# Sparse graph attention on one core: part one as a software pipeline, biases filled into PSUM by ScalarE, and a small tile of 12 slots first

## The chip, the cores and the metric

The kernel runs on one core of one Trainium2 chip. The metric is the device time of one execution in microseconds; of the kernel before it is the median of three runs. The engines are called PE (TensorE, matrix products), DVE (VectorE), ACT (ScalarE), POOL (GpSimd, which also issues the indirect DMAs) and SP (SyncE, which issues DMAs). PE reads its stationary operand by weight loads, which the profile lists as PEld.

## The reference

A layer norm with relu, then graph attention over the neighbours that an adjacency matrix lists, then a residual.

```python
# x: 3327 x 1024, adj: 3327 x 3327 int32 (symmetric, with the diagonal, about 0.5% ones), weights 1024 x 1024
h = jnp.maximum(_layernorm(x, axis=-1), 0.0)
f = h @ Wf + bf
g = h @ Wg + bg
e = relu(f @ g.T)
scores = jnp.where(adj > 0, e, -9e15)
attention = softmax(scores, axis=1)
out = x + attention @ (h @ W + bW)
```

## The kernel before

The kernel uses that a row has few neighbours (37 at most, 17 in the mean). It never forms f, g or the full score matrix. With A = Wf Wg^T the score of nodes i and j is a dot of q_i = h_i A + ... with h_j, and since attention weights sum to 1, attention @ (h W + bW) is (attention @ h) W + bW.

Part one runs over 26 tiles of 128 rows. It loads adj and x, makes h and stores it in DRAM (`hd`), turns each adjacency row into a list of neighbour numbers (`pay`, stored as `pd`), and makes A meanwhile. The list comes from the eight greatest of each of 16 segments of (adj times column number), from which five rounds take the 40 greatest.

```python
def degrees(t):                                   # per tile; ACT, then POOL
    ...
        nc.scalar.activation(r[:n, b:e], a[:n, b:e], AF.Relu, accum_out=to)
        nc.gpsimd.tensor_mul(r[:n, b:e], r[:n, b:e], iotaj[:n, b:e])
def edges(t, r):                                  # DVE
    for s in range(SEG):                          # SEG = 16
        nc.vector.max(cand[:n, s * 8 : s * 8 + 8], r[:n, s * SW : min(N, (s + 1) * SW)])
    ...
    for i in range(0, KM, 8):                     # KM = 40
        nc.vector.max(lst[:n, i : i + 8], cand[:n])
        if i + 8 < KM:
            nc.vector.match_replace(cand[:n], lst[:n, i : i + 8], cand[:n], 0.0)
    ...
for t in range(NT):                               # NT = 26
    r = degrees(t)
    normed(t)                                     # load x, mean, variance, h, store hd
    edges(t, r)
    if t >= LAG: counted(t - LAG)
    ...
    if t < KD: load_Wg(t)
    elif t < 2 * KD: make_A(t - KD)
```

Then the nodes are sorted by degree on DVE and PE (`counted`, ranks, one-hot products), which gives `perm`: slot s holds the 128 nodes of rank 128 s and up. CAPS[s] is the greatest number of neighbours in slot s:

```python
CAPS = [37, 25, 23, 22, 21, 21, 20, 20, 19, 19, 18, 18, 17, 17, 17, 16, 16, 15, 15, 15, 14, 14, 13, 13, 12, 11]
```

Part two runs over the slots, two tiles prepared ahead. For each slot POOL gathers the lists and the h rows of its nodes, PE makes q, and for each neighbour k POOL gathers a row of h for every node, DVE takes the dot, a softmax follows (in two halves where CAPS is over 16), and the rows are summed by their weights, on DVE or on ACT and PE. PE multiplies the sum by W; x is gathered onto the result by an accumulating DMA; the result is scattered to `out`.

```python
def prepare(s):
    gather(pi, pd[:, :], perm[:, s : s + 1])      # lists;  psp has 3 buffers
    gather(hp, hd[:, :], perm[:, s : s + 1])      # own rows; 2 buffers of their own
    transposed2(hT, hp)
    for o in range(0, QW, QB):                    # three q blocks of 342
        for k in range(KD):
            nc.tensor.matmul(ps[:, :QB], hT[:, k, :], A_sb[:, k, o : o + QB], start=(k == 0), stop=False)
        nc.tensor.matmul(ps[:, :QB], ones3, v3[:, o : o + QB], start=False, stop=True)   # bias of q, bf16 in 3 terms
        nc.scalar.copy(q[:, o : o + QB], ps[:, :QB])
    nc.vector.tensor_copy(df, pi[:, KM : KM + 1])
    nc.vector.tensor_scalar(bads[...], df[...], float(CAPS[s]), None, op0=ALU.is_gt)
    ...
def dot(s, k):                                    # G has 25 buffers
    gather(g, hd[:, :], e["pi"][:, k : k + 1])
    nc.vector.tensor_tensor_reduce(junk, g, e["q"][:, :D], 1.0, e["q"][:, D : D + 1], ...)
def on_tensor(s, k0, k1):                         # which rows are summed by ACT and PE
    m = min(max(0, CAPS[s] - 13), k1 - k0 - 2)
    ...
def project(s):
    ...
        for k in range(KD):
            nc.tensor.matmul(ps, yT[:, k, :], W_sb[:, k, o * CB : (o + 1) * CB], start=(k == 0), stop=False)
        nc.tensor.matmul(ps, ones3, bW3[:, o * CB : (o + 1) * CB], start=False, stop=True)   # bias bW
        nc.scalar.copy(r[:, o * CB : (o + 1) * CB], ps)
    gather(r, x[:, :], perm[:, s : s + 1], compute_op=ALU.add)
```

A dense path, taken only if some row doesn't fit CAPS or a segment has over eight neighbours, stands behind a branch and isn't run on these data.

Of the kernel before, what the change touches and what calls it, by code (L numbers as in the profile page):

```python
# [18 lines left out]
EPS = 1e-5  # L19
# [3 lines left out]
NBIN = 64  # L23

CAPS = [37, 25, 23, 22, 21, 21, 20, 20, 19, 19, 18, 18, 17, 17, 17, 16, 16, 15, 15, 15, 14, 14, 13, 13, 12, 11]
ONE_CHUNK = 16
# [263 lines left out]
def edge_path(ctx: ExitStack, tc: tile.TileContext, x, adj, Wf, bf, Wg, bg, W, bW, out, flag):  # L290
# [9 lines left out]

    nc = tc.nc
# [10 lines left out]
    PW = KM + 1  # L312
# [14 lines left out]
    pd = dram.tile([N, PW], I32, name="pd")  # L327

    ident = const.tile([P, P], FP, name="ident")
    make_identity(nc, ident)  # L330
    eps = const.tile([P, 1], FP, name="eps")
    nc.gpsimd.memset(eps, EPS)
    iotak = const.tile([P, KM], FP, name="iotak")
    nc.gpsimd.iota(iotak, pattern=[[1, KM]], base=0, channel_multiplier=0, allow_small_or_imprecise_dtypes=True)
    ones3 = const.tile([3, P], BF, name="ones3")
    nc.gpsimd.memset(ones3, 1.0)
    bads = const.tile([P, NT + 2], FP, name="bads")
# [7 lines left out]
    v3 = wts.tile([3, QW], BF, name="v3")  # L345
    nc.gpsimd.memset(A_sb[:, :, D:], 0.0)
    nc.gpsimd.memset(v3[:, D:], 0.0)
    bW3 = wts.tile([3, O], BF, name="bW3")


    with ExitStack() as part1:
        pool1 = lambda name, bufs, **kw: part1.enter_context(tc.tile_pool(name=name, bufs=bufs, **kw))
        c1 = pool1("c1", 1)
        wrow = pool1("wrow", 3)
        wT = pool1("wT", 2)
        ln = pool1("ln", 5)
        lnj = pool1("lnj", 1)
        kpool = pool1("key", 4)
        cpool = pool1("cand", 2)
        p_tr = pool1("p_tr", 2, space=PSUM)  # L360
        p_mm = pool1("p_mm", 2, space=PSUM)
        p_u = pool1("p_u", 1, space=PSUM)
        p_c = pool1("p_c", 1, space=PSUM)
        p_v = pool1("p_v", 1, space=PSUM)

        iotaj = c1.tile([P, N], FP, name="iotaj")
        nc.gpsimd.iota(iotaj, pattern=[[1, N]], base=1, channel_multiplier=0, allow_small_or_imprecise_dtypes=True)
        iotap = c1.tile([P, P], FP, name="iotap")
        nc.gpsimd.iota(iotap, pattern=[[1, P]], base=0, channel_multiplier=0, allow_small_or_imprecise_dtypes=True)

        held = p_c.tile([P, NBIN + KM], FP, name="held")
        iotad, lst = held[:, :NBIN], held[:, NBIN:]
# [10 lines left out]
        deg = c1.tile([P, NT], FP, name="deg")  # L383
# [4 lines left out]
        nc.gpsimd.memset(deg, 1.0)  # L388
        nc.gpsimd.memset(cnt, 1.0)
# [5 lines left out]
        def normed(t):  # L395

            n = rows(t)
            xt = ln.tile([P, D], FP, name="xt")
            for a, m in pieces(t):
                nc.sync.dma_start(xt[a : a + m], x[t * P + a : t * P + a + m, :])  # L400
            rstd = ln.tile([P, 1], FP, name="rstd")
            nmr = ln.tile([P, 1], FP, name="nmr")
            if t % 2:
                st = ln.tile([P, D // CB, 6], FP, name="st")
                for c in range(D // CB):
                    nc.vector.bn_stats(st[:n, c, :], xt[:n, c * CB : (c + 1) * CB])
                mv = ln.tile([P, 2], FP, name="mv")
                nc.vector.bn_aggr(mv[:n], st[:n])
                nc.scalar.activation(nmr[:n], mv[:n, 0:1], AF.Copy, scale=-1.0)
                nc.scalar.activation(rstd[:n], mv[:n, 1:2], AF.Sqrt, bias=eps[:n])  # L410
            else:
                sums = ln.tile([P, 2], FP, name="sums")
# [6 lines left out]
            nc.vector.reciprocal(rstd[:n], rstd[:n])  # L419
            nc.scalar.activation(nmr[:n], nmr[:n], AF.Copy, scale=rstd[:n])  # L420
            nc.scalar.activation(xt[:n], xt[:n], AF.Relu, bias=nmr[:n], scale=rstd[:n])
            for a, m in pieces(t):
                nc.scalar.dma_start(hd[t * P + a : t * P + a + m, :], xt[a : a + m])

        def degrees(t):
            n = rows(t)
            r = kpool.tile([P, N], FP, name="r")
            a = r.bitcast(I32)
            for b, m in pieces(t):
                nc.sync.dma_start(a[b : b + m], adj[t * P + b : t * P + b + m, :])  # L430

            cuts = [0, SEG // 2 * SW, N] if t >= NT - 2 else [0, N]
            for i, (b, e) in enumerate(zip(cuts, cuts[1:])):
                to = deg[:n, t : t + 1] if not i else half[:n]
                nc.scalar.activation(r[:n, b:e], a[:n, b:e], AF.Relu, accum_out=to)  # L435
                nc.gpsimd.tensor_mul(r[:n, b:e], r[:n, b:e], iotaj[:n, b:e])  # L436
                if i:
                    nc.scalar.activation(deg[:n, t : t + 1], deg[:n, t : t + 1], AF.Identity, bias=half[:n])
            return r

        def edges(t, r):

            n = rows(t)
            cand = cpool.tile([P, SEG * 8], FP, name="cand")
            for s in range(SEG):
                nc.vector.max(cand[:n, s * 8 : s * 8 + 8], r[:n, s * SW : min(N, (s + 1) * SW)])  # L446
            pos = cpool.tile([P, SEG * 8], BF, name="pos")
            nc.vector.tensor_scalar(
                pos[:n], cand[:n], 0.0, None, op0=ALU.is_gt, op1=ALU.add, accum_out=cnt[:n, t : t + 1]
            )  # L450
            for i in range(0, KM, 8):
                nc.vector.max(lst[:n, i : i + 8], cand[:n])
                if i + 8 < KM:
                    nc.vector.match_replace(cand[:n], lst[:n, i : i + 8], cand[:n], 0.0)
            nc.vector.tensor_scalar(lst[:n], lst[:n], float(N), 1.0, op0=ALU.min, op1=ALU.max)
            nc.vector.tensor_scalar(pay[:n, t, :KM], lst[:n], -1.0, None, op0=ALU.add)
            dg = cpool.tile([P, 1], FP, name="dg")
            nc.vector.tensor_scalar(dg[:n], deg[:n, t : t + 1], float(NBIN - 1), None, op0=ALU.min)
            nc.vector.tensor_copy(pay[:n, t, KM : KM + 1], dg[:n])
            nc.vector.tensor_scalar(oh[:n, t, :], iotad[:n], dg[:n], None, op0=ALU.is_equal)  # L460
# [23 lines left out]
        def transposed(to, of):  # L484

            for g in range(0, KD, 4):
                ps = p_tr.tile([P, 4, P], FP, name="ps_tr")
                for k in range(4):
                    nc.tensor.transpose(ps[:, k, :], of[:, (g + k) * P : (g + k + 1) * P], ident)
                nc.scalar.copy(to[:, g : g + 4, :], ps)  # L490

        WgT = c1.tile([P, KD, D], FP, name="WgT")
        bfT = c1.tile([P, KD], FP, name="bfT")
        bgT = c1.tile([P, KD], FP, name="bgT")
        v_ps = p_v.tile([P, KD], FP, name="v_ps")
        cols = c1.tile([P, 2 * KD + 1], FP, name="cols")
        terms = c1.tile([P, 3, 2 * KD + 1], BF, name="terms")
        identb = c1.tile([P, P], BF, name="identb")
        nc.vector.tensor_copy(identb, ident)
        nc.gpsimd.memset(cols, 0.0)  # L500
        nc.gpsimd.dma_start(bfT, bf.rearrange("(k p) -> p k", p=P))
        nc.gpsimd.dma_start(bgT, bg.rearrange("(k p) -> p k", p=P))
        nc.gpsimd.dma_start(cols[:, KD : 2 * KD], bW.rearrange("(k p) -> p k", p=P))

        def load_Wg(c):
            wr = wrow.tile([P, D], FP, name="wr")
            nc.sync.dma_start(wr, Wg[c * P : (c + 1) * P, :])
            transposed(WgT[:, :, c * P : (c + 1) * P], wr)

        def make_A(c):  # L510

            wr = wrow.tile([P, D], FP, name="wr")
            nc.sync.dma_start(wr, Wf[c * P : (c + 1) * P, :])
            WfT = wT.tile([P, KD, P], FP, name="WfT")
            transposed(WfT, wr)
            for o in range(OH):
                ps = p_mm.tile([P, CB], FP, name="ps_A")
                for k in range(KD):
                    nc.tensor.matmul(  # L519
                        ps, WfT[:, k, :], WgT[:, k, o * CB : (o + 1) * CB], start=(k == 0), stop=(k == KD - 1)  # L520
# [34 lines left out]
        for t in range(NT):  # L555
# [3 lines left out]
            if t >= LAG:  # L559
                counted(t - LAG)  # L560
# [300 lines left out]
```

## Time and profile before

| | |
|---|---|
| Time, median of 3 (lowest, highest) | 1366.73 us (1366.68, 1373.93) |
| Span of the profiled execution | 1370.1 us |
| Mean granted PE clock | 0.939 of full |
| DVE, PE busy | 1218.5 us, 1154.2 us |
| POOL, ACT busy | 875.0 us, 489.2 us |
| Moved by DMA | 372.52 MB, mean 272 GB/s |
| Ranking chain on DVE | 272.3 to 284.7 us |
| First dot of part two | 314.4 us |
| Last sum on DVE | ends 1329.4 us |

In the profile a group is read as line, engine, operation, output<-input, shapes, count, then the busy time and the mean of one in ns, then the idle time of its engine just before it and what ended that idle time. "issue" is idle time for which the profile shows no releaser. PE runs an fp32 product of 128 rows in two passes, so its counts are twice those of the code. Busy shares are means over the span; the two parts have different limits, so the tables by stretches of time say more than the totals.

### The profile page before, as it was taken

The page shows a single profiled execution, that of the slowest core. Times are in us where ns is not written, and L with a number is a line of the kernel's source. Part 1 is how long each engine was busy: PE and PEld are TensorE (multiplying, and loading weights), DVE is VectorE, ACT ScalarE, POOL GpSimd, SP SyncE. Part 2 cuts the span into 40 slices and gives each one's busy share as a digit, 9 for nine tenths or more (in the row PEclk, how much of TensorE's full clock was granted, in tenths as well). Part 3 has the DMA queues.
Part 4 walks back from the last instruction along what each step waited for, and adds up shares of the span by engine and source line. Part 5 has one row for each costly group of instructions (what it writes and reads, how often), then busy time and mean ns, then how long its engine had stood idle before and what let it go on. Part 6 is the DMA issues. An engine that isn't in the chain of part 4 may idle for free.

```text
span 1370.1 us, 14184 instructions
## 1 busy us (share of the span) xinstructions
PE 1154.2 (84%) x4355; PEld 676.0 (49%) x4355; DVE 1218.5 (89%) x2595; ACT 489.2 (36%) x774; POOL 875.0 (64%) x628
## 2 busy tenths in 40 slices
PE   4669899246467998999999999999979999999784
PEld 3545454124244564656555555555545555555331
DVE  4888888928869999999999899999999999999970
ACT  6677676501042542344433233333322222221110
POOL 7787778435456766677667767776656667666411
PEclk9999999568689999999999999999999999999897
DMA  9887898268558989898989988988877889888612
GB/s 367 356 336 281 320 351 276 68 257 327 172 166 302 348 294 320 299 334 292 309 290 311 303 269 312 302 294 296 272 240 250 255 281 306 272 271 285 198 32 63
DMA packets 97711, 372.52 MB, mean 272 GB/s; under 512 B 14269, under 2 KB 14685, under 8 KB 94298
## 3 DMA queue, kind: packets, MB, share of 16 engines
q0 software_dynamic: 79552, 286.85, 62.4%
q1 hardware_dynamic: 10860, 70.49, 13.6%
q10 hardware_dynamic: 7212, 14.18, 2.9%
q8 instruction: 36, 0.59, 0.2%
q14 instruction: 51, 0.41, 0.1%
HBM read 343.67 MB, written 27.80 MB: 271 GB/s over the span
## 4 chain that ended last, share of the span: by engine, by line
PE 43%; issue 14%; DVE 9%; DMA 4%; POOL 4%; ACT 2%; POOLq 0%; ACTq 0%; DVEq 0%
PE ps_q L666 18%; PE ps_o L758 17%; PE yT_ps L724 6%; DVE G L746 5%; DMA G<-hd,pi 4%; POOL G L637 3%; DVE junk L683 3%; PE ps_q L667 1%; PE ps_o L759 1%; ACT hT L650 1%; DMA pi<-pd,perm 1%; PE ps_t L649 1%; DVE sc L683 1%; POOL res L637 0%; ACT q L668 0%
## 5 line engine op out<-in xcount | busy, mean ns | idle before, releaser
L637 POOL DMA_INDIRECT G<-hd,pi x468 | 541.2, 1156 | 220.2 <-issue 93.5
L683 DVE CUSTOM_DVE_ANT_0 junk<-G,q 128x1024 bf16<-128x1024 f32 x468 | 599.4, 1281 | 35.3 <-ACT q L668 18.1
L666 PE MATMUL ps_q<-A_sb,hT 128*128 128x342 f32 x1248 | 399.2, 467 | 59.4 <-ACT q L668 41.8
L746 DVE SCALAR_TENSOR_TENSOR G<-G,sc 128x1024 f32<-128x1024 f32 x320 | 410.8, 1284 | 4.6 <-ACT G L744 4.1
L758 PE MATMUL ps_o<-W_sb,yT 128*128 128x512 f32 x832 | 374.8, 604 | 4.4 <-ACT yT L753 4.4
L666 PEld LDWEIGHTS ps_q<-A_sb,hT 128*128 128x128 f32 x1248 | 231.8, 194 | 177.6 <-ACT q L668 43.7
L758 PEld LDWEIGHTS ps_o<-W_sb,yT 128*128 128x128 f32 x832 | 156.5, 192 | 195.4 <-issue 182.3
L436 POOL TENSOR_TENSOR r<-r,iotaj 128x3327 f32<-128x3327 f32 (+4 forms) x28 | 188.6, 6743 | 66.6 <-ACT r L435 51.7
L724 PE MATMUL yT_ps<-ident,G 128*128 128x128 f32 x1184 | 146.2, 279 | 24.7 <-DVE sc L708 8.2
L446 DVE MAX8 cand<-r 128x8 f32<-128x208 f32 (+2 forms) x416 | 134.4, 361 | 35.2 <-POOL r L436 35.2
L724 PEld LDWEIGHTS yT_ps<-ident,G 128*128 128x128 f32 x1184 | 133.8, 143 | 41.8 <-issue 15.7
L760 ACT COPY res<-ps_o 128x512 f32<-128x512 f32 x52 | 30.4, 585 | 298.9 <-PE ps_o L759 298.9
L740 ACT ACTIVATE G<-G,sc 128x1024 f32<-128x1024 f32 x122 | 129.2, 1135 | 0.0
L668 ACT COPY q<-ps_q 128x342 f32<-128x342 f32 x78 | 33.5, 447 | 244.8 <-DVE sc L683 135.9
L519 PE MATMUL ps_A<-WgT,WfT 128*128 128x512 f32 x256 | 118.5, 623 | 2.7 <-ACT WfT L490 2.6
L637 POOL DMA_INDIRECT res<-in_x_dram,perm x26 | 46.2, 1776 | 67.4 <-ACT res L760 62.8
L519 PEld LDWEIGHTS ps_A<-WgT,WfT 128*128 128x128 f32 x256 | 50.6, 200 | 65.1 <-issue 61.2
L768 POOL DMA_INDIRECT out_dram<-res,perm x25 | 34.5, 1378 | 72.5 <-DMA res<-in_x_dram,perm 72.5
L435 ACT ACTIVATE r<-r 128x3327 f32<-128x3327 int32 (+4 forms) x28 | 77.5, 2768 | 0.1
L650 ACT COPY hT<-ps_t 128x512 f32<-128x512 f32 x52 | 28.9, 590 | 59.2 <-PE ps_t L649 32.0
L637 POOL DMA_INDIRECT hp<-hd,perm x26 | 26.8, 1032 | 35.0 <-DVE final L612 21.2
L649 PE MATMUL ps_t<-ident,hp 128*128 128x128 f32 x208 | 31.2, 292 | 15.7 <-issue 10.8
(137 smaller groups left out, 743.9 us busy)
## 6 DMA issues: line engine op xcount, KB each, us to landing
r<-in_adj_dram SPq DMA_DIRECT2D x25, 1663.5 KB, 9.0
xt<-in_x_dram SPq DMA_DIRECT2D x25, 512.0 KB, 9.8
hd<-xt ACTq DMA_DIRECT2D x25, 512.0 KB, 6.8
G<-hd,pi POOLq DMA_INDIRECT x468, 6.1
wr<-in_L_gnn_Wg_dram SPq DMA_DIRECT2D x8, 512.0 KB, 13.9
wr<-in_L_gnn_Wf_dram SPq DMA_DIRECT2D x8, 512.0 KB, 9.6
W_sb<-in_L_gnn_W_dram SPq DMA_DIRECT2D x1, 4096.0 KB, 16.3
r<-in_adj_dram SPq DMA_DIRECT2D x1, 1455.6 KB, 8.8
```

What stands on the lines that cost most here:

```text
L435: nc.scalar.activation(r[:n, b:e], a[:n, b:e], AF.Relu, accum_out=to)
L436: nc.gpsimd.tensor_mul(r[:n, b:e], r[:n, b:e], iotaj[:n, b:e])
L446: nc.vector.max(cand[:n, s * 8 : s * 8 + 8], r[:n, s * SW : min(N, (s + 1) * SW)])
L519: nc.tensor.matmul(ps, WfT[:, k, :], WgT[:, k, o * CB : (o + 1) * CB], start=(k == 0), stop=(k == KD - 1))
L637: return nc.gpsimd.indirect_dma_start(out=to, out_offset=None, in_=table, in_offset=bass.IndirectOffsetOnAxis(ap=idx, axis=0), **kw,)
L649: nc.tensor.transpose(ps[:, k, :], of[:, (g + k) * P : (g + k + 1) * P], ident)
L666: nc.tensor.matmul(ps[:, :QB], hT[:, k, :], A_sb[:, k, o : o + QB], start=(k == 0), stop=False)
L683: nc.vector.tensor_tensor_reduce(junk, g, e["q"][:, :D], 1.0, e["q"][:, D : D + 1], op0=ALU.mult, op1=ALU.add, accum_out=e["sc"][:, k : k ...
L724: nc.tensor.matmul(e["yT"][:, c, :], g[:, c * P : (c + 1) * P], ident, is_transpose=True, start=(first and c % 4 == 0), stop=(last and c % ...
L740: nc.scalar.activation(g, g, AF.Copy, scale=p)
L746: nc.vector.scalar_tensor_tensor(y, g, p, y, op0=ALU.mult, op1=ALU.add)
L758: nc.tensor.matmul(ps, yT[:, k, :], W_sb[:, k, o * CB : (o + 1) * CB], start=(k == 0), stop=False)
```

## The change

Part one becomes a software pipeline over the tiles, with more buffers and a fixed order of each engine's steps. The lists keep only the 24 greatest; the candidates that are left are stored in DRAM (`cd`), and the two slots with over 24 neighbours take the rest from there. A's product and the bias of q (`vb`, one row for all partitions) come from one set of 342-wide products. In part two the bias matmuls go: ACT copies the bias into the PSUM bank before the matmuls[...]. One more row in most slots is summed on ACT and PE. In the last tile x is gathered ahead and added by DVE. The slot of 12 neighbours (24) is moved to the front, and its dots are made in three column pieces, each as its q block is known.

```diff
-NBIN = 64
+KL = 24
+MORE = 2
+NBIN = 48
+ORDER = [24, *range(24), 25]
...
-        ln = pool1("ln", 5)
-        kpool = pool1("key", 4)
+        ln = pool1("ln", 6)
+        kpool = pool1("key", 5)
+        candp = pool1("candp", 4)
...
-        for t in range(NT):
-            r = degrees(t)
-            normed(t)
-            edges(t, r)
+        for i in range(NT + 3):
+            empty(lambda e: e[0] < i)
+            if i < NT:
+                load(i)
+                (Wg in the first four tiles)
+                degrees(i)
+                keys(i)
+                measured(i)
+            late = NT - 2
+            if i - 3 < late and i >= 3:
+                scaled(i - 3)
+            ...
+            if i and i <= NT:
+                edges(i - 1)
+            ...
+            if i >= 3:
+                left(i - 3)                       # candidates to cd
+            (counted, store_lists, and four steps of A's making per block of A)
...
         nc.vector.scalar_tensor_tensor(cand[:n, upper], pos[:n, upper], float(HW), cand[:n, upper], ...)   # added
-            for i in range(0, KM, 8):
+            for i in range(0, KL, 8):
...
+        slots, has: whether each row's degree fits its slot, once after the ranking
...
-    psp = ctx.enter_context(tc.tile_pool(name="ps", bufs=3))
-    gpool = ctx.enter_context(tc.tile_pool(name="G", bufs=25))
-    hpool = ctx.enter_context(tc.tile_pool(name="hp", bufs=2))
+    psp = ctx.enter_context(tc.tile_pool(name="ps", bufs=2))
+    gpool = ctx.enter_context(tc.tile_pool(name="G", bufs=26))
...
+    def filled(pool, name, row, w, at):
+        ps = pool.tile([P, CB], FP, name=name)
+        if at < 2:
+            nc.tensor.matmul(ps, ident, A_sb[:, 0, :CB], start=True, stop=True)
+        o = at * w % row.shape[1]
+        nc.scalar.copy(ps[:, :w], row[:, o : o + w])
+        banks[name, at] = ps
...
     def prepare(s):
-        hp = hpool.tile([P, D], FP, name="hp")
+        hp = gpool.tile([P, D], FP, name="G")
...
-                nc.tensor.matmul(ps[:, :QB], hT[:, k, :], A_sb[:, k, o : o + QB], start=(k == 0), stop=False)
-            nc.tensor.matmul(ps[:, :QB], ones3, v3[:, o : o + QB], start=False, stop=True)
+                nc.tensor.matmul(ps[:, :QB], hT[:, k, :], A_sb[:, k, o : o + QB], start=False, stop=(k == KD - 1), ...)
             nc.scalar.copy(q[:, o : o + QB], ps[:, :QB])
-        nc.vector.tensor_copy(df, pi[:, KM : KM + 1])
-        nc.vector.tensor_scalar(bads[: rows(s), s : s + 1], df[: rows(s)], float(CAPS[s]), None, op0=ALU.is_gt)
+            if at + 2 < 3 * NT:
+                filled(p_q, "ps_q", vb, QB, at + 2)
...
+        if s >= MORE:
+            return
+        gather(ct, cd[:, :], perm[:, s : s + 1])  # then three more rounds: neighbours 25 to 40
...
+    def dots_of_first(s, cap):
+        for k in range(cap):
+            st["gathered"] = gather(G[s, k], hd[:, :], e["edges"][k])
+        for i, o in enumerate(range(0, D, QB)):
+            for k in range(cap):
+                nc.vector.tensor_tensor_reduce(junk[:, :w], G[s, k][:, o : o + w], e["q"][:, o : o + w], ...)
+        nc.vector.tensor_reduce(e["sc"][:, :cap], sums.rearrange("p c k -> p k c"), AX.X, ALU.add)
...
-        m = min(max(0, CAPS[s] - 13), k1 - k0 - 2)
+        m = min(max(0, CAPS[s] - 12), k1 - k0 - 2) if s != ORDER[0] else (k1 - k0) // 2
...
-        gather(r, x[:, :], perm[:, s : s + 1], compute_op=ALU.add)
+        if s < NT - 1:
+            gather(r, x[:, :], perm[:, s : s + 1], compute_op=ALU.add)
+        (in the last tile: nc.vector.tensor_tensor(r, ps, e["x"], op=ALU.add))
```

## The prediction

> **What bounds the kernel now.** I read the busy time by stretches first, because the page's shares average over two quite different parts. Each row gives the stretch in us, its length, the busy us of PE, its weight loads, DVE, ACT and POOL (with counts), the granted clock, the DMA share and GB/s.
>
> ```profile
> 0.00:50.00 50.00, 23.55 (x105) 21.77 (x105) 30.58 (x127) 31.40 (x44) 37.38 (x33) 1.00 0.98 384
> 200.00:250.00 50.00, 41.43 (x167) 22.60 (x165) 43.73 (x210) 34.21 (x55) 37.06 (x7) 0.93 0.68 229
> 250.00:300.00 50.00, 10.30 (x68) 7.42 (x69) 32.68 (x130) 12.65 (x25) 15.41 (x11) 0.50 0.40 142
> 350.00:400.00 50.00, 20.95 (x67) 12.17 (x65) 41.45 (x60) 3.34 (x9) 26.08 (x19) 0.69 0.60 195
> 600.00:700.00 100.00, 95.69 (x373) 55.12 (x374) 99.86 (x154) 34.34 (x54) 71.83 (x62) 1.00 0.92 317
> 1100.00:1200.00 100.00, 99.12 (x343) 54.64 (x342) 98.63 (x146) 24.16 (x43) 69.26 (x59) 1.00 0.87 284
> 1300.00:1370.00 70.00, 45.09 (x111) 19.58 (x109) 27.69 (x31) 7.21 (x13) 8.39 (x6) 0.85 0.20 47
> ```
>
> To 285 us is part one, the neighbour lists: no engine is full, and DMA is full only at first (0.98, then 0.68). From 314 us part two runs, 468 dots and 320 sums on DVE. From 450 to 1300 DVE and PE are both full: neither alone is the bound. Between 250 and 450, and after 1310, both stand partly empty. Second, the chain of waits (shares of the span), which names PE and hardly ACT:
>
> ```profile
> PE 43%; issue 14%; DVE 9%; DMA 4%; POOL 4%; ACT 2%; POOLq 0%; ACTq 0%; DVEq 0%
> ```
>
> Third, the groups of part two, for the unit costs; then timeline rows of one q block and of the end.
>
> ```profile
> L683 DVE CUSTOM_DVE_ANT_0 junk<-G,q 128x1024 bf16<-128x1024 f32 x468 | 599.4, 1281 | 35.3 <-ACT q L668 18.1 <-DMA G<-hd,pi 15.6
> L746 DVE SCALAR_TENSOR_TENSOR G<-G,sc 128x1024 f32<-128x1024 f32 x320 | 410.8, 1284 | 4.6 <-ACT G L744 4.1
> L740 ACT ACTIVATE G<-G,sc 128x1024 f32<-128x1024 f32 x122 | 129.2, 1135 | 0.0
> L667 PEld LDWEIGHTS <-ones 3*128 3x128 bf16 x78 | 7.1, 91 | 35.6 <-issue 35.6
> L759 PEld LDWEIGHTS <-ones 3*128 3x128 bf16 x52 | 4.7, 90 | 39.4 <-issue 39.4
> ```
>
> ```profile
> 303.68 4.87 PE L666 MATMUL ps_q<-A_sb,hT 128*128 128x342 f32 x16
> 308.48 0.31 PE L667 MATMUL ps_q<-v,ones 3*128 3x342 bf16 x1
> 308.73 4.87 PE L666 MATMUL ps_q<-A_sb,hT 128*128 128x342 f32 x16
> ...
> 1351.68 1.55 POOL L637 DMA_INDIRECT res<-in_x_dram,perm x1 [9.03 <-ACT res L760]
> 1358.22 1.01 POOL L768 DMA_INDIRECT out_dram<-res,final x1 [4.99 <-DMA res<-in_x_dram,perm]
> ```
>
> The bias matmul looks like 0.31 us, but the weight load before it waits about 0.47 us ("issue"). A q block starts every 5.05 us; 16 passes at the spacing of their weight loads (4.32 us for the first 15 and a load) need 4.56, so the bias costs 0.48 us of PE. An output half starts every 7.4 us where its 16 passes need about 6.85: 0.54 us.
>
> [...] The trace before has no such write; its nearest row is the ACT copy of 128x342 out of PSUM, 447 ns. [...] in 250 to 300 us the granted clock is 0.50, and weight loads at 343 us come every 0.57 us instead of 0.285. [...] The 1024-wide dot takes 1.276 us[...]. [...] the fullest 25 us here moved 421 GB/s, the first 50 us 384.
>
> **Part one, lists.** Its queue becomes a software pipeline: loads first, statistics, scaling and edges of earlier tiles after them, with 5 key buffers for 4 and 6 row buffers for 5. In each tile DVE loses two of five MAX8/MATCH_REPLACE rounds (0.29 + 0.27 + 0.08 us each) and three small ops (0.19, 0.13, 0.15), and gains one of about 0.2: 1.28 + 0.47 - 0.2 = 1.55 us, by 26 tiles 40 of about 220 us (232 busy to 285 us, less the ranking chain). PE loses the one-column matmuls. ACT stays near 181 us busy, and issues some 27 candidate stores more at 0.33 us: near 205 with all issues. POOL keeps 26 x 7.36 = 191 us. DMA carries adj 44.3 + x 13.6 + hd 13.6 + two weights 8.4 + lists and candidates 2 = 82 MB; at 384 GB/s that is 213 us. So the floor moves from DVE to DMA and ACT together: I take 222 us for loading, 15 us for the last tile's keys and edges, and the ranking chain on DVE. That chain ran from 272.3 to 284.7; it gains a product and a reduction on 676 elements (0.86 each, half of it under PE's wait) and shrinks 1664 to 1248 elements in two ops (2 x 0.47): 13 us. Perm is ready at 250, not 284.7: **-35 us**.
>
> **First tile of part two.** After perm the gathers of lists and rows must land (before: 12 us to the first matmul; now 14.5, a candidate gather stands ahead), then three q blocks of 6.8, 5 and 5 us. Before, dots began at 314.4 and twelve were over at 330.3, perm + 45.6. Now a third of each dot may begin a block earlier: [...] The first twelve gathers issue 1.24 us apart from perm + 10 and land by perm + 29, so the first step ends there[...]: perm + 44. On DVE that is a draw: about **-2 us**. Its worth is on PE: six of the tile's twelve rows are summed on PE early, while before PE had only 98 of 150 us busy from 300 to 450 and met its first transposed sum at 401.6, behind a tile with 37 slots on 25 buffers.
>
> **The rest of part two.** PE: bias out, 26 x (3 x 0.48 + 2 x 0.54) = 65 us; sums moved to PE go from 122 to 146 (one more in slots 6 to 23, six in slot 24), 24 x 8 passes of 0.137 = 26: PE **-39 us** of 957. DVE: 24 sums fewer at 1.20 us (the pair dot-plus-sum repeats every 2.40) = -29; no df cast and bads test, 26 x 0.25 = -6; two re-sorts of candidates +3; x added on DVE in the last tile +1[...]: **-31 us** net of that. ACT gains 130 fills, 78 x 0.45 + 52 x 0.59 = 66 us, and 24 x 1.1 = 27 of scaling; at 35% busy they should lie beside, though each must pass between a bank's copy and its next block (1 us inside a 4.6 us block). In a late tile such as slot 17 before, PE's 34 us (3 x 5.05 + 2 x 7.4 + 4 x 1.1) and DVE's 27 x 1.2 + 1.3 = 33.7 match the 34 us between tiles; both fall about 1.3, so the pace really falls. Counting forward: perm 250 + 44 + 752 remaining sums and dots x 1.20 (902) + 26 x 1.25 + 5 of small ops (38) + stalls 25 (before 30) = 1259 for DVE's end, against 1329.4: the stretch loses 71 - 35 = **-36 us**, the draw of the first tile included.
>
> **Tail.** DVE's end to the span's end took 41 us. The last tile's x, gathered early and added by DVE, removes the gather-add: 1358.22 - 1351.68 = 6.5 us, and a bias pair 1 us: 33 left, **-8 us**. Sum: -35 - 36 - 8 = -79, and 1366.7 - 79 = 1288; I say **1287 us**.
>
> **Rivals.** (a) Part one stays latency-bound: SP waits before were 64 us on edges to free key buffers, and ACT is one strict line of stores, roots and copies at 205 of 225 us. If only 12 of the 35 come, 1310. For it: four engines now end within 25 us of each other; against it: the deeper buffers and the later scaling take away just the waits named (ACT for rstd 26 us, POOL for ACT 52 us). (b) ACT becomes the waited-for engine in part two, fills queued behind copies that wait for q's release (136 us before, up to 40 at once), so PE waits for filled banks: the -39 is lost and the pace stays with PE, 1315. Against it: p_q already needed that same copy before. (c) Buffers: the gathered rows of a tile's own nodes now share the 26 with neighbours, and the lists have 2 buffers, not 3; gathers stall again around the 37-slot tile, +10: about 1297. (d) Better than I think: DMA at 420 GB/s and fewer stalls at 300 to 450, 1258.
>
> **Range and chances.** (a) alone or (b) alone stays under 1339; only both with (c) would come near. The range is **1258 to 1316**; faster by over 2% 0.95, within 2% 0.04, slower 0.01.
>
> **What would show it.** Right: the ranking done near 250; q blocks 4.6 us apart, output halves 6.9; 340 us sees PE transposed sums; DVE near 99% from 350 on; no x gather after the last output copy. Wrong: ps_q or ps_o matmuls waiting for ACT fills; DMA below 0.85 in part one; DVE idle while PE is full, which would make PE the sole bound; or an end within 1% of before, which would mean the stretches share a limit I have not seen.

## The result, and the profile after

The changed kernel takes 1332.06 us in the median of four runs (1327.41 to 1335.3); the kernel before took 1367.78 beside it. The ratio is 0.9727, with a 95% interval of 0.9685 to 0.977: 36 us less, where 79 had been predicted. The time lies outside the range, 16 us above its upper end.

First the busy time by stretches of the changed kernel, with the columns as in the prediction.

```profile
200.00:250.00 50.00, 29.00 (x94) 17.22 (x93) 45.20 (x199) 32.74 (x55) 34.87 (x10) 0.75 0.58 191
350.00:400.00 50.00, 15.23 (x68) 11.18 (x69) 45.09 (x67) 8.92 (x14) 29.95 (x21) 0.61 0.66 211
600.00:700.00 100.00, 94.03 (x382) 59.69 (x380) 99.68 (x158) 42.77 (x71) 66.53 (x61) 0.98 0.90 306
1100.00:1200.00 100.00, 80.66 (x281) 49.34 (x280) 81.05 (x120) 26.36 (x49) 57.92 (x50) 0.90 0.72 232
1300.00:1331.50 31.50, 17.14 (x46) 7.65 (x44) 1.38 (x2) 2.18 (x4) 3.55 (x3) 0.83 0.20 53
```

The middle (600 to 700 us) is as before: DVE 99.7 of 100 us busy, PE 94.0. The stretch from 1100 to 1200 us is new. DVE was 98.63 us busy there and is 81.05 now, and PE fell with it from 99.12 to 80.66: both stand still together, so something else is waited for. The granted PE clock there went from 1.00 to 0.90. Part one ends earlier; the ranking is written at 259.4 us (before 284.7).

The chain of waits can be followed back from the end only to 956 us in this trace (to 331 us before), so its shares add up to 27% of the span, and to 76% before. PE holds 6 of the 27; it held 43 of the 76:

```profile
issue 7%; DVE 7%; PE 6%; DMA 4%; POOL 2%; ACT 1%; POOLq 0%; ACTq 0%; DVEq 0%
```

The groups of part two, in the form of the prediction, give the unit costs:

```profile
L767 DVE CUSTOM_DVE_ANT_0 junk<-G,q 128x1024 bf16<-128x1024 f32 x456 | 586.5, 1286 | 8.8 <-DMA G<-hd,pi 4.3 <-ACT q L735 0.8
L848 DVE SCALAR_TENSOR_TENSOR G<-G,sc 128x1024 f32<-128x1024 f32 x296 | 381.4, 1289 | 10.6 <-ACT G L846 6.8 <-ACT G L812 2.7
...
L711 ACT COPY ps_q<-vb 128x342 f32<-128x342 f32 x78 | 34.8, 447 | 7.3 <-DMA pd<-pay 5.2
L711 ACT COPY ps_o<-bWb 128x512 f32<-128x512 f32 x52 | 30.7, 592 | 1.3
```

Dots and sums are each 5 ns longer than before (1281 and 1284). The fills take 447 and 592 ns on ACT. The timeline shows what they buy: successive copies of q, one for each block, start 4.60 us apart, where the blocks were 5.05 apart.

```profile
1136.85 0.45 ACT L735 COPY q<-ps_q 128x342 f32<-128x342 f32 x1 [3.46 <-PE ps_q L731]
...
1141.45 0.45 ACT L735 COPY q<-ps_q 128x342 f32<-128x342 f32 x1 [3.67 <-PE ps_q L731]
...
1146.05 0.45 ACT L735 COPY q<-ps_q 128x342 f32<-128x342 f32 x1 [3.68 <-PE ps_q L731]
```

The end, from the same view, has no gather of x after the last sum. DVE adds x, once for each output half (the two are 6.87 us apart, where the prediction had 6.9), and the scatter follows within a microsecond:

```profile
1311.24 0.69 DVE L866 TENSOR_TENSOR res<-ps_o,G 128x512 f32<-128x512 f32 x1 [13.07 <-PE ps_o L861]
...
1318.11 0.69 DVE L866 TENSOR_TENSOR res<-ps_o,G 128x512 f32<-128x512 f32 x1 [6.17 <-PE ps_o L861]
1319.08 1.01 POOL L881 DMA_INDIRECT out_dram<-res,final  x1 [8.31 <-DVE res L866]
```

What stands still at 1100 to 1200 us is in the list of waits (who waited for whom: us in total, times, the longest):

```profile
POOL G L686 <- DVE G L848: 67.9, 47, 11.2
PE ps_t L698 <- DMA G<-hd,perm: 67.5, 5, 42.6
...
DVE rs L807 <- ACT sc L800: 19.1, 7, 6.2
```

G<-hd,perm is the gather of a tile's own rows, which in the changed kernel takes its buffer from the 26 of the neighbours' rows. PE waited 67.5 us for five of them; before, where own rows had two buffers to themselves, it waited 5.0 us once. DVE waited 19.1 us for ACT's exponentials (before 0.7). The timeline shows how the two hang together; these rows are from three engines of one stretch:

```profile
1111.78 1.51 PE L698 MATMUL ps_t<-ident,G 128*128 128x128 f32 x6 [8.59 <-DMA G<-hd,perm]
...
1123.33 0.59 ACT L870 COPY res<-ps_o 128x512 f32<-128x512 f32 x1 [6.74 <-PE ps_o L861]
1123.95 0.59 ACT L711 COPY ps_o<-bWb 128x512 f32<-128x512 f32 x1
1124.48 0.30 ACT L800 ACTIVATE sc<-sc,nm 128x15 f32<-128x15 f32 x1
...
1124.90 0.16 DVE L807 RECIPROCAL rs<-l 128x1 f32<-128x1 f32 x1 [6.25 <-ACT sc L800]
...
1129.24 1.74 POOL L686 DMA_INDIRECT G<-hd,pi  x1 [11.21 <-DVE G L848]
```

PE stands 8.59 us for a late own row and is late with everything after it. ACT stands 6.74 us at a copy of PE's output. In these rows the next exponential comes after that copy and the fill that follows it, and DVE waits 6.25 us for it. While DVE waits it frees no buffers, and GpSimd's next gather waits 11.21 us. My reading is that this makes the next own row late again; five are late in all. I call this the jam.

### The profile page after: what moved, and what is told of

It reads as the page before. It is cut to its first block, busy times and chain, and to the rows that moved or that the text cites. A ratio compares the mean times of both kernels' runs of the same rounds, so it can differ in the third digit from the quotient of the medians.

```text
span 1331.5 us, 14117 instructions
## 1 busy us (share of the span) xinstructions
PE 1105.4 (83%) x4312; PEld 690.2 (52%) x4312; DVE 1184.0 (89%) x2377; ACT 580.1 (44%) x923; POOL 847.2 (64%) x677
## 5 line engine op out<-in xcount | busy, mean ns | idle before, releaser
L686 POOL DMA_INDIRECT G<-hd,pi x454 | 487.4, 1074 | 199.2 <-issue 102.6
L848 DVE SCALAR_TENSOR_TENSOR G<-G,sc 128x1024 f32<-128x1024 f32 x296 | 381.4, 1289 | 10.6 <-ACT G L846 6.8
L424 POOL TENSOR_TENSOR r<-r,iotaj 128x1664 f32<-128x1664 f32 (+3 forms) x52 | 191.6, 3724 | 31.9 <-ACT r L417 31.8
L826 PE MATMUL yT_ps<-ident,G 128*128 128x128 f32 x1376 | 172.5, 281 | 28.6 <-DVE G L848 15.3
L826 PEld LDWEIGHTS yT_ps<-ident,G 128*128 128x128 f32 x1376 | 155.8, 144 | 55.3 <-ACT G L842 26.4
L842 ACT ACTIVATE G<-G,sc 128x1024 f32<-128x1024 f32 x146 | 154.9, 1136 | 0.0
L551 PE MATMUL ps_A<-WgT,WfT 128*128 128x342 f32 x432 | 140.5, 485 | 0.2 <-ACT WfT L532 0.2
L551 PEld LDWEIGHTS ps_A<-WgT,WfT 128*128 128x128 f32 x432 | 86.3, 205 | 60.5 <-issue 21.1
L698 PE MATMUL ps_t<-ident,G 128*128 128x128 f32 x208 | 31.9, 303 | 80.1 <-DMA G<-hd,perm 67.5
L698 PEld LDWEIGHTS ps_t<-ident,G 128*128 128x128 f32 x208 | 27.3, 157 | 88.8 <-issue 74.5
```

The source lines that it names most:

```text
L424: nc.gpsimd.tensor_mul(r[:n, b:e], r[:n, b:e], iotaj[:n, : e - b])
L551: nc.tensor.matmul(ps[:, :QB], WfTs[c][:, k, :], WgT[:, k, o : o + QB], start=(k == 0), stop=(k == KD - 1))
L686: return nc.gpsimd.indirect_dma_start(out=to, out_offset=None, in_=table, in_offset=bass.IndirectOffsetOnAxis(ap=idx, axis=0), **kw,)
L826: nc.tensor.matmul(e["yT"][:, c, :], g[:, c * P : (c + 1) * P], ident, is_transpose=True, start=(first and c % 4 == 0), stop=(last and c % ...
L842: nc.scalar.activation(g, g, AF.Copy, scale=p)
L848: nc.vector.scalar_tensor_tensor(y, g, p, y, op0=ALU.mult, op1=ALU.add)
```

## The experiments

Four theories were set up. **Theory 1**: own rows in the shared ring of buffers come late, and that stops PE, ACT and DVE in turn. **Theory 2**: ACT's strict order, with the fills in it, delays the exponentials whatever the own rows do. **Theory 3**: too many rows were moved to PE, so that the late tiles wait for PE and for buffers. **Theory 5**: part one is held by loads that wait for stores. There is no theory 4; the new beginning of part two is tested by e3 and e4. In the table "ranked" is when the ranking is written in the profiled run. "Stretch" runs from the end of the first dots on DVE (twelve; in the kernel before too) to DVE's last sum, and is split into DVE's busy and idle time; it is left empty where a run bears on part one alone. Times are us.

| run | what differs from the changed kernel | median | ratio to before (95%) | ranked | stretch = busy + idle |
|---|---|---|---|---|---|
| before | | 1367.8 | | 284.7 | 999.1 = 969.7 + 29.4 |
| changed | | 1332.1 | 0.9727 (0.9685 to 0.977) | 259.4 | 991.3 = 949.6 + 41.7 |
| e1 | own rows apart, 1 buffer | 1330.2 | 0.9709 (0.9669 to 0.975) | 257.2 | 989.9 = 950.4 + 39.5 |
| e2 | own rows apart, 2 buffers | 1321.9 | 0.9645 (0.9604 to 0.9687) | 258.6 | 988.0 = 949.0 + 39.0 |
| e17 | e2 again | 1323.7 | 0.9677 (0.9649 to 0.9705) | 257.5 | 981.2 = 948.7 + 32.5 |
| e3 | plain order, whole dots, 6 sums back to DVE | 1341.6 | 0.9781 (0.9733 to 0.9829) | 259.7 | 1003.3 = 957.3 + 46.0 |
| e4 | whole dots in the first tile | 1328.5 | 0.9699 (0.9658 to 0.974) | 258.7 | 991.9 = 949.0 + 42.9 |
| e5 | bias matmul, no fills | 1341.6 | 0.979 (0.975 to 0.9829) | 258.3 | 1002.1 = 958.7 + 43.4 |
| e16 | e2 with bias matmul, no fills | 1332.2 | 0.9729 (0.9703 to 0.9756) | 262.0 | 993.7 = 956.1 + 37.6 |
| e6 | 18 sums back to DVE | 1367.9 | 0.9988 (0.9967 to 1.0009) | 258.7 | 1024.9 = 964.4 + 60.5 |
| e9 | e2 and 18 sums back to DVE | 1330.0 | 0.9704 (0.9671 to 0.9736) | 258.9 | 987.3 = 964.9 + 22.4 |
| e10 | e2 and 14 more sums on PE | 1329.8 | 0.9703 (0.9671 to 0.9735) | 260.5 | 989.1 = 945.3 + 43.8 |
| e7 | 8 row buffers in part one | 1329.0 | 0.9682 (0.9638 to 0.9726) | 256.4 | |
| e8 | product earlier | 1335.6 | 0.9767 (0.9709 to 0.9825) | 262.9 | |
| e12 | lists unsorted | 1332.7 | 0.9724 (0.9694 to 0.9754) | 259.7 | |
| e11 | e2, e4 and e7 together | 1317.9 | 0.9612 (0.9584 to 0.9641) | 257.5 | 985.5 = 948.7 + 36.8 |

The runs e13 to e15 stood on a chip on which the kernel before took 1422 us, so only their part one is used.

Two things limit what the last two columns can say, since each comes from one execution. The changed kernel and all variants in the table but e7, e8, e11 and e12 have the same part one, and yet their ranking was written between 257.2 and 262.0 us. And e2 and e17 are the same kernel: the profiled executions took 1328.9 and 1320.6 us, with DVE busy 949.0 and 948.7 us and idle 39.0 and 32.5. So a few us of idle time, or of the ranking, tell nothing; DVE's busy time repeats.

### Own rows apart: e1, e2, e17

```diff
(cut to what changes)
-gpool: G, bufs=26            hp = gpool.tile(... "G")
+gpool: G, bufs=25 (e1) or 24 (e2, e17)
+hpool: hp, bufs=1 (e1) or 2 (e2, e17)       hp = hpool.tile(... "hp")
```

> The changed kernel (1332 us), with the rows of a tile's own nodes in a buffer of their own again (one), and 25 buffers for neighbours' rows instead of 26: the same memory. Theory 1 (the own rows stand in the neighbours' ring and come late, PE and then DVE stand still for them at 342 to 412 us and at 960 to 1200 us): the waits of ps_t for the own rows fall from 67 us to under 10, DVE's busy share in 1100 to 1200 us goes from 0.81 to over 0.95, the time falls by 15 to 30 us, to 1302 to 1317. Theory 2 (ACT's strict order with the fills delays the exponentials, whatever the own rows do): within 5 us of 1332. Theory 3 (too few buffers for the neighbours altogether): slower by 2 to 8 us, 1334 to 1340.

> As the run before, with two buffers for own rows and 24 for neighbours' rows. Theory 1: if the second buffer matters, another 0 to 5 us faster than with one; if the neighbours' ring matters, 0 to 8 us slower than with one. Theory 2: within 5 us of 1332. Theory 3: 1338 to 1348.

> The control: own rows in two buffers and the fills, as in e2, 1318 to 1326 us.

One buffer gained nothing that can be told from noise (1330.2). The stop at 1100 to 1200 us is gone (DVE 99.83 of 100 us busy, where it was 81.05), but PE still waits 21.0 us for own rows: the next gather now waits until PE has transposed the last one (18.0 us of GpSimd's time), and new idle time of DVE appears earlier (from 500 to 800 us it is busy 283.2 us, against 298.7). With two buffers the time is 1321.9 and, repeated, 1323.7: 8 to 10 us less from the same memory. Part of theory 1's 15 to 30 us is there. In e17 PE no longer waits for an own row to land, and DVE's wait for exponentials falls from 19.1 to 3.1 us, although all the fills are still in ACT's line. So theory 2 is no cause of its own: the late own row comes first, and ACT's order passes it on. The stretches of e17 show DVE (third pair) full where it had stood still:

```profile
900.00:1000.00 100.00, 98.15 (x384) 58.89 (x382) 97.87 (x150) 40.94 (x69) 64.71 (x57) 1.00 0.83 274
1000.00:1100.00 100.00, 93.23 (x342) 55.89 (x343) 97.07 (x139) 33.45 (x56) 68.52 (x56) 0.98 0.87 284
1100.00:1200.00 100.00, 95.03 (x341) 56.85 (x339) 97.69 (x139) 32.69 (x58) 67.96 (x57) 0.98 0.84 279
```

DVE is busy 292.6 of these 300 us; in the changed kernel it was 271.6, and in e2 291.2. The longest wait of all, PE's 42.6 us near 342 to 385 us, stopped DVE hardly at all: DVE was busy 41.2 of these 43 us with the dots and sums of the 37-slot tile. In the 65 us after it DVE stands 7.4 us. No run takes that stop away, so its price is not shown. In e17 PE stands 34.5 us in the same place, now for the fill of a q bank, and DVE is no fuller (42.57 against 45.09 of the 50 us from 350). PE's waits for fills in e17 are these (nine, 34.5 us the longest):

```profile
PE ps_q L732 <- ACT ps_q L712: 51.7, 9, 34.5
```

### Rows moved to PE: e6, e9, e10

```diff
-m = min(max(0, CAPS[s] - 12), k1 - k0 - 2)
+m = min(max(0, CAPS[s] - 13), k1 - k0 - 2)     # e6, e9; - 11 in e10
```

> The changed kernel with as many rows summed on PE as before (slots less 13 in place of 12): 18 sums go back to DVE. My prediction's step (DVE bounds[...]): slower by 15 to 22 us, 1347 to 1354. Theory 3 (the late tiles are held by PE and by late buffers, and more rows on ACT and PE only hold buffers longer): same or faster by up to 10 us, 1322 to 1334.

> Own rows in two buffers of their own (24 for neighbours), and the 18 sums back on DVE. With the shared ring, giving the 18 sums back cost 36 us (1332 to 1368)[...]. Theory 1 (the rest was own rows standing late in the shared ring): [...] 1336 to 1346, and no wait of ps_t for own rows over 10 us. Rival (a row on DVE costs twice what I count, whatever the ring): 1353 to 1363.

> Own rows in two buffers, and one more row per tile summed on PE (slots less 11 in place of 12), 19 or 20 sums off DVE. If DVE still sets the pace: 20 us less, 1302 to 1312. If PE or ACT do by now (PE 97 of 100 us busy in the middle): 1318 to 1335.

e6 missed every expectation: 18 sums back on DVE cost 36 us and undo the whole gain. DVE's work explains 964.4 - 949.6 = 15 of it. The idle time, 60.5 us against 41.7, lies where own rows come late, now from 900 us on (stretches and wait of e6):

```profile
900.00:1000.00 100.00, 81.57 (x293) 48.68 (x291) 85.18 (x135) 32.02 (x58) 59.34 (x50) 0.91 0.77 255
1000.00:1100.00 100.00, 84.94 (x299) 51.37 (x299) 88.15 (x124) 29.60 (x50) 58.13 (x48) 0.91 0.73 228
1100.00:1200.00 100.00, 85.03 (x286) 50.74 (x285) 84.58 (x122) 28.52 (x52) 60.89 (x51) 0.90 0.77 245
```

```profile
PE ps_t L698 <- DMA G<-hd,perm: 99.2, 11, 43.8
```

Eleven own rows are late here, not five. e9 settles it. It differs from e6 only in where own rows lie, and it takes 1330.0: 38 us less, with 22.4 us of idle time. Theory 1 and its rival were 1336 to 1346 and 1353 to 1363; the result is even below the former. So the shared ring costs 38 us with this split of rows and 8 to 10 with the changed kernel's. The changed kernel had half hidden its own fault by moving one more row per tile to PE. That this frees buffers earlier is my reading; no run shows it by itself.

With own rows apart, those 18 sums are worth only 6 to 8 us (1330.0 against 1323.7 and 1321.9), not the 15 to 22 I had expected, and one more step of the same kind (e10, 14 sums more; I had expected 19 or 20) loses 6 to 8. Two things use the gain up. First, DVE's busy time falls only 16.2 us (964.9 to 948.7), 0.90 us a sum. A sum between two dots starts 1.20 us after its neighbour, while a dot next to a dot, or a sum next to a sum, starts 1.32 to 1.33 after it (rows of the changed kernel):

```profile
1101.54 1.28 DVE L848 SCALAR_TENSOR_TENSOR G<-G,sc 128x1024 f32<-128x1024 f32 x1
1102.74 1.27 DVE L767 CUSTOM_DVE_ANT_0 junk<-G,q 128x1024 bf16<-128x1024 f32 x1
...
1111.83 1.28 DVE L767 CUSTOM_DVE_ANT_0 junk<-G,q 128x1024 bf16<-128x1024 f32 x1
1113.16 1.28 DVE L767 CUSTOM_DVE_ANT_0 junk<-G,q 128x1024 bf16<-128x1024 f32 x1
```

In the instruction order as built, DVE has 184 such neighbours of one kind in e9, 220 in e17 and 356 in e10: take sums away and the dots lose their partners. In e10 the 14 sums less free only 3.4 us of DVE's busy time. Second, idle time grows, from 22.4 us in e9 to 32.5 and 39.0 in e17 and e2 and 43.8 in e10. Theory 3, right about the direction for the wrong kernel, fits from here on; which wait takes this time is not shown.

### Fills: e5, e13, e16

```diff
-nc.scalar.copy(ps[:, :w], row[:, o : o + w])        # fill, then start=False
+nc.tensor.matmul(ps[:, :QB], ones3, zeros3[:, :QB], start=False, stop=True)   # and for ps_o
```

> The changed kernel (1332 us) with its 130 fills by ACT taken out and a bias matmul of 3 rows back in every q block and output half (the rows hold zeros here, so the biases are left out of the result; the work is that of the kernel before). My prediction: the fills take 65 us from PE, and PE and DVE bind together, so PE's return to 962 us costs 20 to 35 us: 1352 to 1367. Theory 2 (the fills in ACT's strict order delay the exponentials): faster by 3 to 10 us, 1322 to 1329. Rival (PE's freed time lies beside DVE's work, DVE alone bounds): within 8 us, 1324 to 1340.

> Own rows in two buffers (1322), fills out and a bias matmul of 3 rows of zeros back in each block (the biases are left out of the result). With the jam this cost 9.6 us. If PE's freed time was worth what I predicted and the jam hid it: 20 to 35 us, 1342 to 1357. If DVE alone bounds nearly everywhere: 5 to 12 us, 1327 to 1334.

> Own rows in two buffers, fills out and a bias matmul of 3 rows of zeros back in each block (the biases are left out of the result), beside its control e17. If PE's freed time was worth what I predicted and the jam hid it: 20 to 35 us slower than the control, 1342 to 1357. If DVE alone bounds nearly everywhere: 5 to 12 us slower, 1327 to 1334.

The rows held zeros, as the biases of these data do, so nothing is lost. e5 is 9.6 us slower than the changed kernel, e16 8.5 slower than e17 on the same chip (1329.88 to 1334.71 against 1320.55 to 1327.11). Both fit "DVE alone bounds nearly everywhere" and neither fits my 20 to 35. The jam did not hide the fills' worth; it was never there.

Even the 8.5 to 9.6 us need not be PE's time. Between e17 and e16 PE's busy time after the ranking rises by 45 us (931.5 to 976.9), and DVE's in the stretch by 7.4, though DVE's dots and sums are the same. The edit also changed the built order on DVE: 272 neighbours of one kind in e16 against 220 in e17, and 298 in e5 against 240 in the changed kernel. At 0.13 us each that is 7 us and 7.5 us, an estimate from the spacings above, and most of what was lost. What the fills are worth with DVE's order held fixed is not shown. They also take ACT's time; the two effects are measured together. Of e13 only the ratio to its own kernel before stands, 0.9762 (0.9649 to 0.9876), too wide to add anything.

### The beginning of part two: e3, e4

```diff
-dots_of_first(ORDER[0], CAPS[ORDER[0]])        # e3 and e4: whole dots instead
-ORDER = [24, *range(24), 25]                   # e3 only
+ORDER = [*range(26)]
-m = ... if s != ORDER[0] else (k1 - k0) // 2   # e3 only: six rows of slot 24 go back from PE to DVE
```

> The changed kernel with the tiles in their plain order, the 37-slot tile first, and whole dots: the new beginning of part two taken away. My prediction's step: the first tile is a draw on DVE of 2 us and gives PE early work: slower by 3 to 15 us, 1335 to 1347. Rival: the first 12-slot tile only puts the 37-slot tile, and its jam of buffers, second, where it makes PE wait 42.6 us: the plain order is faster by 5 to 15 us, 1317 to 1327.

> The changed kernel with the 12-slot tile still first, but with whole dots in place of the three steps of a third. If the steps do what they are for (dots begin two q blocks earlier, at the price of 22 us of pieces instead of 16 us of dots): the first tile's dots end 2 to 6 us later than perm + 47.9, the time 1332 to 1338. Rival: the gathers' 1.28 us each set the first step's end, and the pieces' extra 6 us is lost: same or up to 4 us faster, 1328 to 1332.

The small tile first, with six of its rows summed on PE, is worth 9.5 us (e3), or 13 against e4, which has it with whole dots. It was set at 2 us and "early work on PE", and its six sums were priced among the 24 moved to PE. Not all of the 13 us comes from the order: in e3 the six sums are back on DVE (302 sums against 296), and DVE's busy time is 8.3 us longer than in e4 (957.3 against 949.0), while the first twelve dots end 3.2 us later and idle time is 3.1 us longer. So the order without the six rows is worth less than these figures; how much less is not shown. The three steps bring nothing. In e4 the first dot begins at 287.26 us, and twelve whole dots are over at the ranking + 44.5 us. The 36 pieces begin at 279.9 but are over at the ranking + 47.6, because the first step ends only when the twelfth row lands (292.1) and two full steps, 14.3 us, follow. So the rival expectation, that the gathers set the end of the first step, came true. The 3.5 us between the medians lie within the spread of the runs; the 3.1 us of the traces point the same way.

### Part one: e7, e8, e12, e14, e15

```diff
e7, e15: -ln = pool1("ln", 6)              +ln = pool1("ln", 8)
e8, e15: -T1 = NT - 1                      +T1 = NT - 4        # the product's last tile
e12:     -match_replace between the rounds of each list   (the lists repeat their first entries)
e14:     -keys of the second half of the columns          (the lists hold wrong indices)
```

> The changed kernel with eight buffers for the rows of x in part one in place of six. Theory 5 (the loads wait for the normalised rows to be stored, 94 us in the queue's waits, and that sets the end of part one): those waits fall below 40 us, the ranking is done at 249 to 254 us instead of 259, the time falls 5 to 10 us. Rival (DMA's rate of some 366 GB/s and the last tiles' keys and edges set it): the ranking stays at 257 to 260 us and the time within 3 us of 1332.

> The changed kernel with the product of the two weights spread over three tiles fewer in part one, so that it is over before the last tiles. In the changed kernel ACT reaches the last tile's degrees only at 229.1 us, behind a copy of the product that waits 3.8 us for PE, while the last tile's numbers are there by about 217. If ACT's strict order sets the end of part one: the ranking is done 3 to 8 us earlier, at 251 to 256, and the time falls by as much. Rival (POOL's keys and DVE's edges of the last three tiles, each about 8 us, set it): 257 to 261, time within 3 us of 1332.

> The changed kernel with the two match-and-replace rounds of each tile's list left out of part one (the list then holds its first eight entries three times, so the result is not the reference's; nothing else changes). It takes some 0.3 us x 2 x 26 = 14 to 18 us from DVE in part one and nothing from DMA. If DVE's work per tile sets part one's pace: the ranking is done 6 to 14 us earlier, at 245 to 253 us. If DMA and the loads set it: 257 to 260.

> The changed kernel with the keys of the second half of each tile's columns left out on GpSimd (the lists then hold wrong indices; nothing else changes): its work in part one falls from 191 to 96 us. If its line sets the end of part one: the ranking is done at 235 to 250 us instead of 259. If DMA and ACT's order do: 256 to 260.

> The three changes together (1318), and the product of the weights three tiles earlier. If the loads and ACT's order hide each other's effect: the ranking at 247 to 253 us (with eight row buffers alone 257), time 1309 to 1314. If GpSimd's line sets it: 256 to 260, 1316 to 1320.

More buffers cut the loads' wait for stores from 94 to 25 us, while their wait for DVE's candidates rose from 11 to 36, and the ranking came at 256.4. With the earlier product it came at 262.9, and with both (e15) at 258.1. These three lie in or within 1 us of the 257.2 to 262.0 that unchanged part ones show. 15.5 us less busy time on DVE (e12) moved nothing: 259.7. Only half of GpSimd's keys left out (e14) moved the ranking clearly, to 249.6; on the same chip e13, with part one unchanged, had 258.3. The stretches of e14 (GpSimd is the fifth pair, then clock, DMA share, GB/s) show what comes next:

```profile
50.00:100.00 50.00, 43.83 (x161) 29.15 (x161) 43.11 (x182) 40.72 (x65) 25.62 (x7) 1.00 0.99 399
100.00:150.00 50.00, 43.06 (x172) 28.52 (x171) 47.98 (x212) 41.26 (x64) 22.73 (x7) 0.97 0.99 386
```

So theory 5 falls: of what was tried, the line of GpSimd's keys alone sets part one's end, and for some 9 us only, with DMA right behind it (0.99 busy). GpSimd's rows of the changed kernel add up to it: it begins at 14.7 us, works 191 us, waits 31.8 us for ACT's degrees, and ends at 238.2. ACT's degrees are thus a part of this line:

```profile
198.09 29.41 POOL L424 TENSOR_TENSOR r<-r,iotaj 128x1664 f32<-128x1664 f32 x8 [4.03 <-ACT r L417]
230.88 7.36 POOL L424 TENSOR_TENSOR r<-r,iotaj 127x1664 f32<-127x1664 f32 x2 [3.38 <-ACT r L417]
```

### A better version: e11

Own rows in two buffers, whole dots in the first tile and eight row buffers, as in the diffs above.

> Three changes that looked good alone, together: own rows in two buffers (1322), whole dots for the first tile (1328.5 against 1332), eight row buffers in part one (1329 against 1332). If they add: 1322 - 3.5 - 3 = 1315.5, 1311 to 1320. If they overlap: 1319 to 1324.

1317.86 us (1315.8 to 1320.12), ratio 0.9612 (0.9584 to 0.9641): it beats both kernels and lies in the range for gains that add (1311 to 1320), 5.9 us below e17 on the same chip. What each of the two small gains is worth alone stays within the spread of the runs.

## Why the prediction was wrong

The direction was right, and the size was off by more than half. In terms of the profiled run my working gave ranking 250 + first tile 44 + remaining dots and sums 940 + stalls 25 + tail 33 = 1292 us. The profile has 259.4 + 47.6 + 949.6 + 41.7 + 33.2 = 1331.5. The 39.5 us between them lie in the first four terms, one by one.

**Part one, -35 (measured -25).** The failed step is "the floor moves from DVE to DMA and ACT together", with GpSimd's 191 us listed and then left out of the floor. The stage waits for GpSimd's line of keys, which ended at 238.2 us, although loading was over well before (DMA 0.58 busy from 200 to 250). What follows took what I had said: 9.2 us for the last tile's edges, and 12.0 for the ranking chain against my 13. My 250 is almost the 249.6 that e14 reaches with half of GpSimd's line gone. Rival (a) named the danger, a latency-bound stage, but the wrong engines. A smaller error in the same step did no harm: I took DVE's saving as a sum of durations, 40 us, where busy time fell only 21 (232.5 to 211.1). The instructions there overlap (in the trace of before their durations up to 272 us add up to 285 us, DVE's busy time to 221.7), so a sum of durations is more than the time they take, and DVE was not the bound anyway.

**First tile, -2 (measured +2).** Perm + 44 became perm + 47.6 (before: perm + 45.6). "The first twelve gathers land by perm + 29": they landed by perm + 33. They were issued a little earlier than I had said (the twelfth at perm + 22.8), but the twelfth landed 9.9 us after its issue, where it took 6.8 before. How long the pieces take was my estimate in perm + 44: the trace of before has no dot of that width. In the changed kernel 24 pieces of 342 elements took 0.516 us each, and 12 of 340 took 0.573. The worth of starting with this tile I saw on PE and did not put into the sum; e3 gives 9.5 us for it together with its six sums.

**Rest of part two, -34, which with the first tile's -2 makes the -36 (measured -8: the stretch from first dots to last sum went from 999.1 to 991.3).** The unit costs on PE hold (q blocks 4.60 us apart), and in this kernel no matmul of q or of the output waited for a fill. That a matmul with start=False adds onto what ACT wrote was my assumption. The trace has the fills (447 and 592 ns) and, with no bias matmul, the matmuls onto them; but the biases of these data are zero, so that a fill other than zero is added is not shown here, and neither is what the one matmul into each bank ahead of its first fill does for it. PE's busy time from the ranking on fell by 31 us, where I had -39. The step that failed is "the pace really falls" for PE and DVE together:

- The fills: by the spacing of its blocks PE lost some 63 us (78 x 0.45 + 52 x 0.53), and the time fell by at most 8.5 to 9.6 (e5, e16), of which some 7 us, by estimate, go with DVE's changed order. DVE sets the pace nearly everywhere, and PE's 43% of the old chain was a tie between two full engines, not a price.
- DVE's busy time was 949.6 us instead of 940, and that these are so close is luck: two errors nearly cancel. I priced the 752 dots and sums at 1.20 us each, 902 us, though in the trace of before the first tile's twelve dots in a row start 1.33 us apart. In the changed kernel's trace 240 of them follow one of their own kind, which at 0.13 us each adds 31 us by estimate; they kept DVE busy 932.8 us. All the small operations added only 16.8 us, not 38. "Sums at 1.20" was the wrong price too: a sum taken from between dots freed 0.90.
- The stalls were 41.7 instead of 25. Rival (c) named the place, own rows in the shared buffers, at +10 "around the 37-slot tile". The size was nearly right for this kernel (8 to 10 us) and the place was wrong: the jam that costs lies at 900 to 1200 us, and at the 37-slot tile DVE went on working. What I did not see is that it is unstable, 38 us with 18 rows more on DVE. With own rows apart, 32.5 (e17) and 39.0 us (e2) of idle time are left, and 22.4 in e9 with fewer rows on PE. That PE then binds is a guess from these runs, not shown wait by wait.

Rival (b), banks waiting for fills, did not come in the changed kernel. With own rows apart PE does wait for fills, 51.7 us in e17, most of it beside the 37-slot tile, and that kernel is faster all the same. What is true in (b) is ACT's order, which hands a late own row on to DVE.

**Tail, -8.** Right: 33.2 us against 33.

The range failed because the rivals were treated as alternatives: 1310 for (a), 1297 for (c). Part one's shortfall, the fills' missing worth and the ring came at once, and they add.

## What to carry to other kernels

When two engines are both full, work taken from one of them may be worth little until the other falls too (here some 63 us of PE gave at most 9.6); price a change by leaving it out of the changed kernel, not by the busy time it frees, and look whether that edit also changed the order of the pacing engine. A buffer that is needed early by one consumer does not belong in a ring whose releases depend on that consumer's later work: with the same memory, two buffers apart were worth 8 to 38 us, and one was worth nothing. Judge a wait by whether the pacing engine stands still beside it: during the longest wait here (42.6 us on PE) DVE was busy 41.2 of 43 us, and the ones of 5 to 9 us stopped it.

## What the runs showed that was not expected

DVE's cost of a 1024-wide pass depends on its neighbour in these traces: 1.20 us when dot and sum alternate, 1.32 to 1.33 when two of a kind follow one another, so that ten sums in a row take 13.17 us. e16 and e17 have the same dots and sums, but 272 against 220 neighbours of one kind in the order as built, and e16's stretch is 12.5 us longer; 52 x 0.13 = 7 of them are these neighbours, and the rest stays open. Giving 18 sums back to DVE cost 36 us with own rows in the shared ring of buffers, and 6 to 8 with own rows apart. And one chip ran the kernel before in 1422 us. In e13, which ran there, part one took the same 258.3 us and DVE's busy time was the same (957.0 us, e16 956.1), but DVE stood idle 86.0 us instead of 37.6, for a reason that no run here shows.
